# Which engines follow the source's order in the first attention: TensorE alone, or TensorE and ScalarE

## The chip, the cores and the metric

The kernel runs on one core of a Trainium2 chip. A core has a matrix engine (TensorE, PE in the profile), a vector engine (VectorE, DVE), a scalar engine (ScalarE, ACT), a general engine (GpSimd, POOL), and a queue that issues transfers (SyncE, SP). Each engine takes its own instructions in one fixed order and meets the others through semaphores. The metric is the device time of one execution in microseconds (us), smaller is better; the kernel before takes 1862.88 us, the median of three runs (1862.3 to 1863.4).

## What is computed

The reference is a block of four layers over `x` of 4 x 512 x 512. The change lies in the first: layer norm, then attention with 16 heads of 32, rotated and normalised queries and keys, and a residual.

```python
x = x + _L0_attn_ref(_layernorm(x), W_qkv, W_o)       # first attention
x = x + _L0_ffn_ref(_layernorm(x), w1, w3, w2)        # weights made ternary
x = x + _L1_attn_ref(_layernorm(x), ...)              # a state-space scan
x = x + _L1_ffn_ref(x, ...)                           # attention, then experts

# _L0_attn_ref
q = q * cos + _rotate_half(q) * sin ; q = _rms_norm(q)   # the same for k
scores = einsum('bhqd,bhkd->bhqk', q, k) / sqrt(D)       # causal
out = einsum('bhqk,bhkd->bhqd', softmax(scores), v)
return einsum('btc,oc->bto', out, W_o)

# _L0_ffn_ref
s = mean(abs(w)) ; w1q = clip(round(w / s), -1, 1) * s   # also w3, w2
```

## The kernel before

Everything is one function, `block_kernel`, fully unrolled. A scheduler orders the instructions of each engine from the source and an estimate of its own of when each becomes ready; inside `tc.manual_schedule(engines=...)` the named engines keep the order of the source instead. The first attention stands in such a block (L400) that names TensorE alone; the three later blocks of this kind are not touched.

The first attention goes over four sequences `b`. For each:

- `norm` and `turn_in`: VectorE makes the normalised `row` (L123) of a tile of 128 tokens, TensorE transposes it (`tp`, L132), ScalarE copies it out to `hT` (L133).
- `project(b, t, s)`, for 4 tiles `t` and `s` = 0, 1, 2 for queries, keys and values: eight matmuls in the profile, `pq` (L284). Values are copied out by ScalarE (`v`, L289). Queries and keys go through a chain over three engines: VectorE makes `rot` (L296, two instructions) and `qk` (L300), GpSimd adds them (L303), ScalarE squares the sum (`sqk`, L305), VectorE sums the squares (`qkss`, L306).
- `scale_heads(b, i)`: nine small VectorE instructions for the inverse roots (L312 to L323) and two large multiplications (L325), for two tiles.
- `turn_heads(b, t)`: two transposes (`tp`, L132) that ScalarE copies out to `qkT` (L133).
- `attend(b, between)`: 16 steps `m`. A step has `scores` (matmuls `sc`, L359, into two PSUM pairs; ScalarE's two exponentials `pt`, L364; GpSimd's causal mask, L365), then what `between[m]` lists, then `weigh` of the step before (matmuls `av` and `sm`, L377). After every fourth `weigh` VectorE takes a reciprocal `r` (L385) and makes `oT` (L386).
- `back(b, t)`: the output projection `y` (L340) and the residual (L343).

The two PSUM pairs serve one step's scores, so the scores of step m+1 start when the exponentials of step m have read them. Four further banks serve `pq`, `tp`, `y`, `av` and `sm` in turn.

`between` spreads other work over the steps of `attend(b)`: the `back` of sequence b-1 in steps 1 to 4, the projections of b+1 in steps 0 and 5 to 15, `scale_heads` in 9 and 14, `turn_heads` in 12 and 13, and one *job* on the feed-forward weights at most. A job is a measurement by ScalarE (sum of absolute values: `measure`, L234, for w1 and w3; `measure_down`, L252, for w2) or a quantisation by VectorE (`quantize`, L201 and L202). The measurements of w1 belong to steps 1, 3, ..., 15 of `attend(0)`, quantisations of w1 and measurements of w2 alternate in `attend(1)`, the rest of w2 and w3 is measured in `attend(2)`, w3 is quantised in `attend(3)`. All pieces go through two buffers `q_w`; each job issues the transfer of the piece two jobs later on SP (L218), which waits for its buffer. The list of jobs, and so SP's order, is fixed by the source.

The opening, ahead of `attend(0)`, is:

```python
norm(0, 2)
for i in range(2):
    turn_in(0, i)
    for t in (2 * i, 2 * i + 1):
        project(0, t, 0)
        project(0, t, 1)
    scale_heads(0, i)
```

then the four value projections and `turn_heads` of sequence 0, and `norm(1)`, `turn_in(1, ...)`.

Of the kernel before, what the change touches and what calls it, by code (L numbers as in the profile page):

```python
# [46 lines left out]
def block_kernel(ctx: ExitStack, tc: tile.TileContext, a: dict, out: bass.AP):  # L47
# [116 lines left out]
    with tc.tile_pool(name="a_w", bufs=1) as aw, tc.tile_pool(name="a_1", bufs=1) as a1, tc.tile_pool(  # L164
# [65 lines left out]
        def measure(name, n):  # L230
            def job(raw):
                if n == 0:
                    parts[name] = const.tile([P, 2 * NK], F32, tag="q_" + name, name="q_" + name)
                nc.scalar.activation(raw, raw, AF.Abs, accum_out=parts[name][:, n : n + 1])  # L234

            jobs.append((half(name, n), job))
# [29 lines left out]
        def norm(b, pieces=1):  # L266
            normed[b] = []
            layer_norm(a1, xs[b], lambda t, op: normed[b].append(op), pieces)
            inputs_T[b] = a1.tile([P, NK, T], F32, tag="hT", name="hT")
            heads[b] = a1.tile([P, NT, 2 * H, D], F32, tag="qk", name="qk")  # L270
            squares[b] = a1.tile([P, NT, 2 * H], F32, tag="qkss", name="qkss")
            turned_qk[b] = a2.tile([P, 2 * NG, T], F32, tag="qkT", name="qkT")
            values[b] = a2.tile([P, NT, C], F32, tag="v", name="v")

        def turn_in(b, i):
            for t in (2 * i, 2 * i + 1):
                row = a2.tile([P, C], F32, tag="row", name="row")
                normed[b][t](row)
                transpose_into(inputs_T[b], row, t * P)

        def project(b, t, s):
            y = bank("pq")
            for k in range(NK):
                nc.tensor.matmul(  # L284
                    y, inputs_T[b][:, k, t * P : (t + 1) * P], wqkv[:, k, s * C : (s + 1) * C],
                    start=k == 0, stop=k == NK - 1,
                )
            if s == 2:
                nc.scalar.copy(values[b][:, t, :], y)  # L289
                return  # L290

            src = y.rearrange("p (h d) -> p h d", d=D)
            dst = heads[b][:, t, s * H : (s + 1) * H, :]
            rot = a2.tile([P, H, D], F32, tag="rot", name="rot")
            for i in range(2):
                nc.vector.tensor_tensor(  # L296
                    rot[:, :, i::2], src[:, :, 1 - i :: 2],
                    sin[:, t, i::2].unsqueeze(1).to_broadcast([P, H, D // 2]), ALU.mult,
                )
            nc.vector.tensor_tensor(  # L300
                dst, src, cos[:, t, :].unsqueeze(1).to_broadcast([P, H, D]), ALU.mult
            )
            nc.gpsimd.tensor_tensor(dst, dst, rot, ALU.add)  # L303
            sq = a2.tile([P, H, D], F32, tag="rot", name="sqk")
            nc.scalar.activation(sq, dst, AF.Square)  # L305
            nc.vector.tensor_reduce(squares[b][:, t, s * H : (s + 1) * H], sq, AX.X, ALU.add)  # L306

        def scale_heads(b, i):
            rs = a1.tile([P, 2, 2 * H], F32, tag="ri_qk", name="ri_qk")
            v = a1.tile([P, 2, 2 * H], F32, tag="ri_v", name="ri_v")  # L310
            u = a1.tile([P, 2, 2 * H], F32, tag="ri_u", name="ri_u")
            nc.vector.tensor_scalar(  # L312
                v, squares[b][:, 2 * i : 2 * i + 2, :], 1.0 / D, QK_EPS, ALU.mult, ALU.add
            )


            nc.vector.tensor_scalar(
                rs.bitcast(I32), v.bitcast(I32), -0.5, float(0x5F3759DF), ALU.mult, ALU.add
            )
            for _ in range(3):  # L320
                nc.vector.scalar_tensor_tensor(u, rs, -0.5, v, ALU.mult, ALU.mult)
                nc.vector.tensor_tensor(u, u, rs, ALU.mult)
                nc.vector.scalar_tensor_tensor(rs, u, 1.5, rs, ALU.add, ALU.mult)  # L323
            for t in (2 * i, 2 * i + 1):
                nc.vector.tensor_tensor(  # L325
                    heads[b][:, t], heads[b][:, t],
                    rs[:, t - 2 * i, :].unsqueeze(2).to_broadcast([P, 2 * H, D]), ALU.mult,
                )

        def turn_heads(b, t):  # L330
            flat = heads[b][:, t].rearrange("p h d -> p (h d)")
            for s in range(2):
                transpose_into(
                    turned_qk[b][:, s * NG : (s + 1) * NG, :], flat[:, s * C : (s + 1) * C], t * P
                )
# [61 lines left out]
        def do(f, *args):  # L397
            return lambda: f(*args)

        with tc.manual_schedule(engines={mybir.EngineType.PE}):  # L400

            norm(0, 2)
            for i in range(2):
# [6 lines that stand above are left out]
                project(0, 2 * i, 2)  # L410
                project(0, 2 * i + 1, 2)
                turn_heads(0, 2 * i)
                turn_heads(0, 2 * i + 1)
            norm(1)
            turn_in(1, 0)
            turn_in(1, 1)
            w3 = None

            for n in range(2 * NK):
                measure("w1", n)  # L420
            at_step = {(0, 1 + 2 * n): n for n in range(2 * NK)}
            scale_at = {(1, 0): "w1", (2, 10): "w2", (3, 0): "w3"}
            for n in range(2 * NK):
                at_step[1, 1 + 2 * n] = len(jobs)
                quantize(lambda: w1, "w1", n)
                at_step[1, 2 + 2 * n] = len(jobs)
                measure_down(n)
            for n in range(2 * NK):
                if n + 2 * NK < NF:
                    at_step[2, 1 + 2 * n] = len(jobs)  # L430
                    measure_down(n + 2 * NK)
                at_step[2, 2 + 2 * n] = len(jobs)
                measure("w3", n)
            for n in range(2 * NK):
                at_step[3, 1 + 2 * n] = len(jobs)
                quantize(lambda: w3, "w3", n)
            fetch_piece()
            fetch_piece()
            w3 = None
            for b in range(B):  # L440
                between = {m: [] for m in range(18)}
                if b > 0:
                    for t in range(NT):
                        between[1 + t].append(do(back, b - 1, t))
                if b + 1 < B:
                    n = b + 1
                    order = [(0, 0), (0, 1), (1, 0), (1, 1), (0, 2), (2, 0), (2, 1), (1, 2)]
                    order += [(3, 0), (3, 1), (2, 2), (3, 2)]
                    for m, (t, s) in zip([0] + list(range(5, 16)), order):
                        between[m].append(do(project, n, t, s))  # L450
                    between[9].append(do(scale_heads, n, 0))
                    between[12].append(do(turn_heads, n, 0))
                    between[13].append(do(turn_heads, n, 1))
                    between[14].append(do(scale_heads, n, 1))

                for m in range(17):
                    if (b, m) in scale_at:
                        between[m].append(do(find_scale, scale_at[b, m]))
                    if (b, m) in at_step:
                        between[m].append(do(next_job, at_step[b, m]))  # L460
                if b == B - 1:
                    first_mv = const.tile([P, NT, 2], F32, tag="mv", name="mv")
                    for t in range(NT):
                        between[9].append(do(statistics, a1, xs[0], t, first_mv))
                attend(b, between)
                if b + 1 < B:
                    turn_heads(b + 1, 2)
                    turn_heads(b + 1, 3)
                if b + 2 < B:
                    norm(b + 2)  # L470
                    turn_in(b + 2, 0)
                    turn_in(b + 2, 1)
                if b + 2 == B:
                    w3 = place("w3")
            for t in range(NT):
                back(B - 1, t)
# [589 lines left out]
    with tc.tile_pool(name="c_1", bufs=1, reuse_waits="tile") as c1, tc.tile_pool(  # L1066
# [82 lines left out]
        engines = {getattr(mybir.EngineType, e) for e in ("PE", "DVE", "Activation", "Pool", "SP")}  # L1149
# [334 lines left out]
    with tc.tile_pool(name="e_1", bufs=1, reuse_waits="tile") as e1, tc.tile_pool(  # L1484
# [255 lines left out]
        engines = {mybir.EngineType.PE, mybir.EngineType.DVE, mybir.EngineType.Activation}  # L1740
# [64 lines left out]
```

## Time and profile before

One execution was profiled: it took 1863.49 us, of which the span from the first to the last instruction is 1861.8 us.

| stretch (us from the span's start) | what runs | length | TensorE busy | ScalarE busy | VectorE busy |
|---|---|---|---|---|---|
| 0 to 40 | loads and the opening | 40.0 | 28.7 | 10.5 | 26.6 |
| 40 to 80 | rest of the opening, first steps of attend(0) | 40.0 | 37.3 | 21.6 | 21.2 |
| 320 to 360 | end of attend(2) | 40.0 | 38.9 | 15.1 | 20.5 |
| 360 to 400 | attend(3) | 40.0 | 38.4 | 15.3 | 24.8 |
| 400 to 1861.8 | the other three layers | 1461.8 | 1386.3 | 786.2 | 903.1 |

"Busy" is the time in which the engine executes; the granted TensorE clock is listed apart, 1.00 being full speed. In the timelines, an engine's idle time and what ended it stand in brackets behind the first instruction after it. Over the whole span GpSimd is busy for 568.4 us (31%).

### The profile page before, as it was taken

The page shows a single profiled execution, that of the slowest core. Times are in us where ns is not written, and L with a number is a line of the kernel's source. Part 1 is how long each engine was busy: PE and PEld are TensorE (multiplying, and loading weights), DVE is VectorE, ACT ScalarE, POOL GpSimd, SP SyncE. Part 2 cuts the span into 40 slices and gives each one's busy share as a digit, 9 for nine tenths or more (in the row PEclk, how much of TensorE's full clock was granted, in tenths as well). Part 3 has the DMA queues.
Part 4 walks back from the last instruction along what each step waited for, and adds up shares of the span by engine and source line. Part 5 has one row for each costly group of instructions (what it writes and reads, how often), then busy time and mean ns, then how long its engine had stood idle before and what let it go on. Part 6 is the DMA issues. An engine that isn't in the chain of part 4 may idle for free.

```text
span 1861.8 us, 27452 instructions
## 1 busy us (share of the span) xinstructions
PE 1757.1 (94%) x10374; PEld 1094.2 (59%) x10374; DVE 1123.3 (60%) x1812; ACT 938.3 (50%) x1940; POOL 568.4 (31%) x383
## 2 busy tenths in 40 slices
PE   7999999999999998899997989999999999999998
PEld 3434343436777766788886875656556554544444
DVE  6456545557656556999888886574766764222222
ACT  2433442332243526989989867675676652011111
POOL 3221212120112020889887860100000000244441
PEclk9999999999999999999999987999999999999999
DMA  7002300102001122323223200000010007455545
GB/s 245 20 1 72 104 1 1 29 18 71 10 28 43 57 80 68 103 94 104 57 63 112 58 28 1 1 24 1 1 35 24 24 24 246 132 91 91 91 80 141
DMA packets 74630, 115.07 MB, mean 62 GB/s; under 512 B 9546, under 2 KB 34762, under 8 KB 73940
## 3 DMA queue, kind: packets, MB, share of 16 engines
q1 hardware_dynamic: 64996, 90.87, 15.2%
q0 software_dynamic: 8656, 20.32, 6.1%
q8 instruction: 83, 1.36, 0.3%
q10 hardware_dynamic: 848, 2.13, 0.3%
q14 instruction: 47, 0.39, 0.1%
HBM read 83.02 MB, written 33.42 MB: 63 GB/s over the span
## 4 chain that ended last, share of the span: by engine, by line
PE 66%; ACT 10%; DVE 9%; issue 2%; DMA 2%; POOL 1%; DVEq 0%; ACTq 0%; POOLq 0%
PE pgr L1684 7%; PE pg L826 7%; PE ys L1135 4%; PE scd L1369 4%; PE yr L1705 4%; PE pq L284 3%; PE bu L1103 3%; PE y L1309 3%; PE y L844 3%; PE pge L1270 3%; PE bu L1098 3%; PE tpd L1392 2%; PE y L340 2%; ACT pr L1380 2%; PE tp L132 2%
## 5 line engine op out<-in xcount | busy, mean ns | idle before, releaser
L1122 POOL TENSOR_TENSOR hc<-h,cb 128x1024 f32<-128x1024 f32 x128 | 301.3, 2380 | 110.2 <-DVE h L1111 91.0
L1111 DVE TENSOR_TENSOR_SCAN h<-da,bu 128x512 f32<-128x512 f32 x256 | 294.9, 1203 | 24.6 <-PE bu L1103 10.5
L284 PE MATMUL pq<-wqkv,hT 128*128 128x512 f32 x384 | 179.6, 615 | 1.5 <-ACT hT L133 1.5
L1091 ACT ACTIVATE da<-delta_l,am 128x511 f32<-128x511 f32 x256 | 163.4, 709 | 2.4 <-DVE h L1111 2.4
L1380 ACT ACTIVATE pr<-scd,nm 128x128 f32<-128x128 f32 (+3 forms) x256 | 133.4, 531 | 57.4 <-DVE nm L1377 56.2
L826 PE MATMUL pg<-hTh,w 128*128 128x512 f32 (+1 forms) x352 | 146.2, 415 | 1.4 <-ACT hTh L813 0.7
L826 PE MATMUL pg<-hTl,w 128*128 128x512 f32 (+1 forms) x352 | 140.6, 400 | 0.2 <-DVE hTl L814 0.2
L1135 PE MATMUL ys<-ident,hc 128*128 128x128 f32 x1024 | 137.2, 278 | 3.2 <-DVE h L1111 1.4
L1103 PE MATMUL bu<-ident,bu 128*128 128x128 f32 x768 | 132.2, 279 | 7.8 <-ACT bu L1085 7.7
L1684 PE MATMUL pgr<-wgu,gTe 128*128 x304 | 137.1, 593 | 0.0
L1085 ACT ACTIVATE bu<-dxT,bts 128x512 f32<-128x512 f32 x192 | 124.4, 712 | 13.0 <-PE bu L1103 12.6
L284 PEld LDWEIGHTS pq<-wqkv,hT 128*128 128x128 f32 x384 | 71.5, 194 | 94.2 <-issue 84.8
L364 ACT ACTIVATE pt<-sc 128x1024 f32<-128x1024 f32 (+3 forms) x128 | 84.1, 698 | 83.5 <-PE sc L359 81.0
L1369 PE MATMUL scd<-kTd,qTd 32*128 32x512 f32 (+3 forms) x512 | 108.9, 505 | 14.4 <-ACT pr L1380 11.5
L1135 PEld LDWEIGHTS ys<-ident,hc 128*128 128x128 f32 x1024 | 119.3, 144 | 4.4 <-DVE h L1111 1.6
L1098 PE MATMUL bu<-diag_l,dxT 128*128 128x128 f32 x512 | 105.6, 289 | 14.0 <-DVE h L1111 10.3
L1377 DVE TENSOR_REDUCE nm<-scd 128x2 f32<-128x256 f32 (+3 forms) x128 | 105.0, 821 | 2.8
L1392 PE MATMUL tpd<-ident,pr 128*128 128x128 f32 x640 | 102.5, 291 | 2.7 <-ACT hTr L133 0.9
L1098 PEld LDWEIGHTS bu<-diag_l,dxT 128*128 128x128 f32 x512 | 81.7, 195 | 37.1 <-DVE h L1111 19.7
L365 POOL TENSOR_SCALAR_AFFINE_SELECT pt<-pt 128x512 f32<-128x512 f32 x64 | 43.5, 679 | 195.3 <-ACT pt L364 195.3
L1103 PEld LDWEIGHTS bu<-ident,bu 128*128 128x128 f32 x768 | 95.3, 145 | 12.0 <-ACT bu L1085 11.9
L1392 PEld LDWEIGHTS tpd<-ident,pr 128*128 128x128 f32 x640 | 75.3, 146 | 36.4 <-issue 23.0
(337 smaller groups left out, 3182.3 us busy)
## 6 DMA issues: line engine op xcount, KB each, us to landing
cb<-c_rows SPq DMA_DIRECT2D x64, 256.0 KB, 3.2
q_w<-in_w2T SPq DMA_DIRECT2D x20, 256.0 KB, 2.7
diag_l<-diags SPq DMA_DIRECT2D x64, 64.0 KB, 1.9
hrows<-h SPq DMA_DIRECT2D x4, 1024.0 KB, 4.3
acc<-x SPq DMA_DIRECT2D x16, 256.0 KB, 2.0
wgu<-in_r_gate SPq DMA_DIRECT2D x7, 512.0 KB, 9.3
wgu<-in_r_up SPq DMA_DIRECT2D x7, 512.0 KB, 10.0
wdn<-in_r_down SPq DMA_DIRECT2D x7, 512.0 KB, 9.4
```

What stands on the lines that cost most here:

```text
L284: nc.tensor.matmul(y, inputs_T[b][:, k, t * P : (t + 1) * P], wqkv[:, k, s * C : (s + 1) * C], start=k == 0, stop=k == NK - 1,)
L826: nc.tensor.matmul(pg[:rows, i, :], w[:, k, f * P : f * P + rows], part[:, k, :], start=k + m == 0, stop=k + m == NK,)
L1091: nc.scalar.activation(da[:, k, 1:], delta[:, k, 1:], AF.Exp, scale=am[:, k, n : n + 1])
L1098: nc.tensor.matmul(bu[:, :P], loaded[b][1][:, 0, k * P : (k + 1) * P], scaled[b, n][0], start=True, stop=True,)
L1103: nc.tensor.transpose(bu[:, t * P : (t + 1) * P], scaled[b, n][t][:, k * P : (k + 1) * P], ident)
L1111: nc.vector.tensor_tensor_scan(h[:, i, :], decays[b, n][:, 2 * half + i, :], bu, 0.0, ALU.mult, ALU.add)
L1122: nc.gpsimd.tensor_tensor(hc, states.pop((b, n, half)), weighed[b, n].unsqueeze(1).to_broadcast([P, 2, T]), ALU.mult)
L1135: nc.tensor.matmul(sums[b][t][:, k * P : (k + 1) * P], hc[:, i, t * P : (t + 1) * P], ident, is_transpose=True, start=n == 0 and k == 0, s ...
L1369: nc.tensor.matmul(sc[:, i, :w], qT[at, g, t * P : w], kT[at, g, :w], start=True, stop=True)
L1380: nc.scalar.activation(pr[:, i, :w], sc[:, i, :w], AF.Exp, bias=nm[:, i : i + 1], accum_out=sums[b, g][:, t, 2 * p + i : 2 * p + i + 1],)
L1392: nc.tensor.transpose(tp[:, j * P : (j + 1) * P], pr[:, i, j * P : (j + 1) * P], ident)
L1684: nc.tensor.matmul(pg, gT[:, k, :], wgu[:, bass.ds(e, 1), k, :].rearrange("p e o -> p (e o)"), start=k == 0, stop=k == NK - 1,)
```

## The change

ScalarE is added to the engines that keep the source's order in the first attention.

```diff
-        with tc.manual_schedule(engines={mybir.EngineType.PE}):
+
+
+        engines = {mybir.EngineType.PE, mybir.EngineType.Activation}
+        with tc.manual_schedule(engines=engines):
```

No instruction is added or removed, and TensorE's, GpSimd's and SP's orders are the same in both programs, line for line. ScalarE's order differs in its first 220 instructions, VectorE's in its first 310, all of them of the first attention. What moves on ScalarE:

- In the opening, the fourth `sqk` now stands ahead of the second pair of `hT` copies (before: three squares, the two copies, a measurement, then the fourth square). The eight measurements of w1 and the first of w2, which lay between the opening's squares, move to their steps: w1 to `attend(0)`, w2 to `attend(1)`.
- In every step with a projection of queries or keys, `sqk` stands ahead of the next step's two `pt` (before: often between the two, or behind).
- In steps 12 and 13, `sqk` stands ahead of the two `qkT` copies of `turn_heads` (before: behind them).
- In `attend(1)`, the measurements of w2 and w3, which stood close together between the exponentials, are one to every second step; those of w3 and the last of w2 move to `attend(2)`.

On VectorE, the inverse roots of the first `scale_heads` are no longer mixed with rotations, and quantisations of w1 are spread over `attend(1)`. Some PSUM banks are handed on otherwise: in steps 12 and 13 the second `tp` takes the bank of the projection just read by VectorE, and the next projection waits for the copy of the first `tp`.

## The prediction

> **What bounds the kernel.** The change can only act where the first attention runs, so I read a table of stretches first, one row for each of `attend(0)`, `attend(1)` and `attend(2)`, cut where their first scores begin. Columns: start and end, length, busy time and (instructions) of PE, PEld, DVE, ACT, POOL, then granted clock, DMA share, GB/s.
>
> ```profile
> 63.37:151.38 88.01, 83.37 (x529) 34.55 (x528) 47.44 (x80) 34.60 (x57) 22.38 (x25) 1.00 0.00 1
> 151.38:263.38 112.00, 104.11 (x564) 42.94 (x563) 63.88 (x107) 46.94 (x92) 22.19 (x25) 0.95 0.25 73
> 263.38:359.84 96.46, 93.93 (x547) 38.43 (x546) 43.95 (x73) 32.24 (x53) 21.18 (x24) 1.00 0.00 1
> ```
>
> TensorE is busy for 93 to 97% of each; no other engine passes 57%. So TensorE is the bound, and what counts is where it stands idle. `attend(1)` and `attend(2)` hold the same projections and `back` calls, yet differ by 15.54 us and in clock. 3.0 of that is the `turn_in` that only `attend(1)` is followed by (148.44 to 151.46 for the same transposes after `attend(0)`). **12.5 us are lost in `attend(1)`.** Next, what TensorE waited for up to 415 us (total, times, longest):
>
> ```profile
> PE sc L359 <- ACT pt L364: 9.6, 8, 2.9
> PE tp L132 <- ACT qkT L133: 3.2, 8, 0.7
> PE sm L377 <- DVE r L385: 2.8, 2, 1.4
> ```
>
> The two longest of the first row are in `attend(1)`: 178.66 to 181.58 and 208.01 to 210.84. ScalarE's timeline at the first shows what it did instead of exponentials:
>
> ```profile
> 175.36 0.63 ACT L252 ACTIVATE q_w<-q_w 128x512 f32<-128x512 f32 x1 [3.16 <-DVE q_u L201]
> ...
> 179.90 0.63 ACT L252 ACTIVATE q_w<-q_w 128x512 f32<-128x512 f32 x1 [3.81 <-DMA q_w<-in_w2T]
> 180.43 0.19 ACT L252 ACTIVATION_READ_ACCUMULATOR q_w<-q_w 128x1 f32 x1
> 180.53 1.92 ACT L364 ACTIVATE pt<-sc 128x1024 f32<-128x1024 f32 x2
> ```
>
> It sat idle for 3.81 us in front of a measurement whose piece had not landed, with the scores (ended 174.45) waiting behind it. At 208 it is the same with w3. After both, the clock falls:
>
> ```profile
> 177.00:180.40 3.40, 1.66 (x19) 0.57 (x17) 1.86 (x4) 0.50 (x1) 0.00 (x0) 1.00 0.53 180
> ...
> 183.90:187.30 3.40, 3.40 (x6) 1.33 (x5) 3.36 (x4) 2.12 (x4) 0.57 (x1) 0.50 0.32 67
> ...
> 207.80:211.20 3.40, 0.57 (x10) 0.30 (x4) 1.19 (x4) 2.71 (x5) 0.00 (x0) 1.00 0.63 174
> 211.20:214.60 3.40, 3.07 (x9) 1.00 (x6) 3.09 (x10) 3.40 (x8) 0.64 (x1) 0.50 0.56 165
> 214.60:218.00 3.40, 3.40 (x5) 1.35 (x4) 3.40 (x3) 0.49 (x1) 1.49 (x1) 0.50 0.25 89
> ```
>
> **Part 1, removed: the stalls of `attend(1)`, -12.5 us.** In source order one measurement (0.63 + 0.19) stands in every second step, so its piece, issued two jobs (two steps, over 8 us) ahead and 2.9 to 3.1 us on its way, is there; and the exponentials are no longer behind several. Idle 2.9 + 2.8; half clock for 3.4 and 6.8 us, which costs half of them, 5.1; the remaining 1.7 are scores paced by late exponentials (1.83 and 3.3 us where 1.14 is usual), partly offset since `attend(1)` was spared the 1.4 us wait for `r` of the third row, which comes back. What is late next is priced in part 4.
>
> The eight measurements of w1 (0.77 + 0.19) go from the opening's idle time into `attend(0)`, the rest of w2 and w3 into `attend(2)`. ScalarE is busy there for 34.6 of 88 and 32.2 of 96.5 us; a step lasts 5 to 6 us, its ScalarE work (two `pt` of 1.0 at most, `sqk`, one measurement, two `qkT` at times) under 5. I cost them at nothing; were that cover gone, each would cost 0.9. SP's order is the same, each job's transfer is only issued later, and nothing needed soon stands behind them: the next on SP are weights of the second layer.
>
> **Part 2, added: the opening, +5.5 us.**
>
> ```profile
> 27.57 0.63 ACT L305 ACTIVATE sqk<-qk 128x512 f32<-128x512 f32 x1 [3.37 <-POOL qk L303]
> ...
> 28.10 1.07 ACT L133 ACTIVATE hT<-tp 128x512 f32<-128x512 f32 x2
> ...
> 28.73 4.99 PE L284 MATMUL pq<-wqkv,hT 128*128 128x512 f32 x11 [1.47 <-ACT hT L133]
> ...
> 30.26 1.50 POOL L303 TENSOR_TENSOR qk<-qk,rot 128x512 f32<-128x512 f32 x1 [1.53 <-DVE qk L300]
> ...
> 31.79 0.63 ACT L305 ACTIVATE sqk<-qk 128x512 f32<-128x512 f32 x1 [1.87 <-POOL qk L303]
> ```
>
> Today the `hT` copies come after the third square, and TensorE resumes at 28.73. Now they stand behind the fourth, which can't start before 31.79: VectorE's and GpSimd's orders ahead of it are unchanged. So 31.79 + 0.63 + 0.59 (one copy) = 33.0, and TensorE, which has only projections queued that read `hT`, is idle from 27.27 to 33.0: 4.3 us more. 5.7 us idle is twice the idles above, so a half-clock run of 3.4 to 6.8 us follows; it begins within the idle, I take 4.2 us of it behind the restart, 2.1 more. The 0.9 us that TensorE waits at 50.48 behind a `v` copy goes: VectorE's inverse roots and two L325 now run unmixed from 33.2 to 38.4, the last square, by a chain of 4.0 us a projection (0.76 + 0.68 + 1.27 + 0.63 + 0.69) from there, ends by 53.4, before TensorE needs that copy (57). 4.3 + 2.1 - 0.9.
>
> **Part 3, added: squares in front.** In `attend(0)` step 1 there is no `back` to cover: `sqk` ends at 71.64, then both `pt` (0.8 each), so the second half of the next scores starts at 73.25 instead of 72.39: **+0.9**. In `attend(1)` and (2), step 1 has 3.7 us of `back` there: nothing. In steps 5 to 11 the square is done 3.5 us after its projection, the `pt` behind it by 6, and the scores that need them start after 7.5 or more: nothing; with that cover gone, 1 to 2 us a step.
>
> Steps 12 and 13, in `attend(0)`:
>
> ```profile
> 125.53 0.60 ACT L133 ACTIVATE qkT<-tp 128x512 f32<-128x512 f32 x1 [2.07 <-PE tp L132]
> ...
> 126.18 0.66 PE L132 MATMUL tp<-ident,qk 128*128 128x128 f32 x4 [0.69 <-ACT qkT L133]
> ...
> 127.90 0.63 ACT L305 ACTIVATE sqk<-qk 128x512 f32<-128x512 f32 x1 [0.44 <-POOL qk L303]
> ```
>
> Now `qkT` follows the square: 128.53 + 0.6 = 129.1. The second `tp` takes another bank (free at 126.5, +0.4), but the next projection waits for the first `qkT`: 129.1 instead of 128.19. In step 13 the same chain (rotation from 132.8, GpSimd to 135.6, square to 136.2, copy to 136.7) holds the step 14 projection to 136.8 instead of 135.20. So **1.6 us** in each of three sequences, **+4.8**.
>
> **Part 4, added: the last piece of w1, +4.3 us.** In `attend(1)` the sixth measurement of w2 stands behind the step 12 `qkT`: 5.3 us after projection 12 ends. Only then does SP issue the next two transfers, 0.33 apart: the last piece of w1 lands at about 5.3 + 0.5 + 2.9 = 8.7. VectorE's fixed order has its quantisation (0.58 + 0.93) ahead of step 13's rotation, which so ends (0.76 + 0.68) at 11.8 rather than 9.2; `qkT` follows at 14.3, not 11.7: 2.6 us. TensorE is idle there for about 2.2 + 0.8. Whether such an idle costs clock is where **the Trainium skill and the trace differ**. "TensorE: Matmul & The Clock Gate", Part 1, has the clock fall only after a whole idle window of about 3.4 us: by it nothing. In the rows above a stretch with 1.66 us of 3.40 busy, and an idle of 2.9, was followed by half clock. I take the trace: one run of 3.4, +1.7. By the rule the total is 1.7 lower. Bounds for the part: 0 (the piece lands early) and 6 (two runs).
>
> **Sum:** -12.5 + 5.5 + 0.9 + 4.8 + 4.3 = **+3.0 us**. On the profiled run that is 1863.5 + 3.0; the median shown is 0.6 lower, so I forecast 1865.9, and a span of 1864.8. The layers behind start later by the same amount. Bounds of the unknown terms: opening half clock 0 to 3.4 (2.1 taken, from the two runs shown), part 4 as said; together about -0.5 to +6.
>
> **Rivals.**
> - *ScalarE blocks more often than I traced* (slower). An engine in source order holds its exponentials behind every square, so each rotation delayed by a reciprocal (3.36 us on VectorE) becomes a TensorE stall. For: the waits list has VectorE and ScalarE idle for the rotation chain over 40 us each. Against: the margins of part 3. Six such steps at 1 us: 1872.
> - *The clock windows behind fall better* (faster). Mean clock from 400 us to the end is 0.98, so about 4% of 1462 us, 58 us or 17 runs of 3.4, go at half; a later start moves the same short idles against those windows. Each run that drops out saves 1.7, so from four on the result is faster: 1859. For: runs follow idles of under 3 us. Against: it may as well add some, and three runs agree within 1.1 us.
> - *The order on the chip doesn't change.* Excluded: the compiled orders differ.
>
> **Chances.** Forecast 0.55, the blocking rival 0.32, the clock rival 0.13. About 0.2% (3.7 us) can't be told from no change: 1859.2 to 1866.6. The forecast lies near the upper edge: of its 0.55, 0.33 the same and 0.22 slower; the clock rival gives 0.10 faster, 0.03 the same. So faster 0.10, same 0.36, slower 0.54. Range 1860 to 1873, about a tenth outside at each end.
>
> **What would show it.** Right: `attend(1)` some 8 us shorter with a clock near 1.00; TensorE idle from 27 to 33 behind `hT`; a wait of projections for `qkT` three times; half clock shortly after 30. Wrong: a shift of the restart of under 3 us; rows of scores waiting for exponentials in steps 5 to 11; VectorE not waiting for w1's last piece; a changed clock behind 400.

## The result and the profile after

The changed kernel takes **1867.86 us** (median of 7 runs, 1866.4 to 1869.1), the kernel before 1862.67 us beside it: a ratio of 1.0027, 95% interval 1.0018 to 1.0037, which is 5.0 us (3.4 to 6.9) lost. A second set of 15 runs in a later session gave 1.0025 (1.0015 to 1.0036). The profiled execution took 1866.38 us, its span is 1864.7 us.

Three rows of the table of stretches of the changed kernel, cut as before at the first scores of `attend(0)`, `attend(1)` and `attend(2)` (start and end, length, busy time and instructions of PE, PEld, DVE, ACT, POOL, granted clock, DMA share, GB/s):

```profile
68.78:160.60 91.82, 85.11 (x530) 34.91 (x529) 47.60 (x81) 39.74 (x73) 22.25 (x25) 0.98 0.11 30
160.60:265.87 105.27, 98.20 (x563) 40.74 (x562) 64.53 (x106) 38.58 (x72) 22.16 (x25) 0.98 0.16 47
265.87:363.93 98.06, 94.05 (x547) 38.42 (x547) 44.01 (x74) 39.41 (x75) 21.10 (x24) 1.00 0.13 37
```

Set against the rows of before, these rows and the opening give the account up to the second layer:

| part | before | after | difference | predicted |
|---|---|---|---|---|
| opening, to the first scores of attend(0) | 63.37 | 68.78 | +5.41 | +5.5 |
| attend(0) | 88.01 | 91.82 | +3.8 | +2.5 |
| attend(1) | 112.00 | 105.27 | -6.7 | -6.6 |
| attend(2) | 96.46 | 98.06 | +1.6 | +1.6 |
| attend(3), to the first matmul of the next layer | 72.43 | 72.70 | +0.3 | 0 |
| sum | 432.27 | 436.63 | +4.4 | +3.0 |

The change gains in one stretch and pays in three. ScalarE is busy for 5 and 7 us longer in `attend(0)` and `attend(2)`, where the measurements went, and 8 us less in `attend(1)`. The +0.3 of `attend(3)` is one wait of scores for exponentials, 0.87 us instead of 0.60.

What TensorE waited for up to 415 us (total, times, longest), in the changed kernel:

```profile
PE pq L284 <- ACT hT L133: 5.1, 1, 5.1
PE sm L377 <- DVE r L385: 5.1, 3, 2.4
PE sc L359 <- ACT pt L364: 4.5, 5, 1.5
PE tp L132 <- DVE qk L300: 3.5, 3, 1.2
PE pq L284 <- ACT qkT L133: 3.1, 6, 0.7
PE sm L377 <- DVE qk L300: 1.5, 1, 1.5
```

The waits of scores for exponentials have halved (9.6 to 4.5 us). The first row (the opening) has grown from 1.5 to 5.1 us and that of `r` from 2.8 to 5.1; new are rows four and five (steps 12 and 13 of three sequences: one wait for VectorE and two for a copy in each) and the last (behind w1's last piece).

The opening, from the timeline of the changed kernel (start, duration; in brackets the idle time before it and what ended it):

```profile
27.30 0.63 ACT L305 ACTIVATE sqk<-qk 128x512 f32<-128x512 f32 x1 [3.37 <-POOL qk L303]
...
29.99 1.49 POOL L303 TENSOR_TENSOR qk<-qk,rot 128x512 f32<-128x512 f32 x1 [1.53 <-DVE qk L300]
31.52 0.63 ACT L305 ACTIVATE sqk<-qk 128x512 f32<-128x512 f32 x1 [3.58 <-POOL qk L303]
32.05 1.07 ACT L133 ACTIVATE hT<-tp 128x512 f32<-128x512 f32 x2
...
32.68 1.22 PE L284 MATMUL pq<-wqkv,hT 128*128 128x512 f32 x1 [5.12 <-ACT hT L133]
```

ScalarE does nothing for 3.58 us, with the copies of finished transposes queued behind a square that waits for GpSimd; TensorE, which needs the copies, starts at 32.68 instead of 28.73.

And the two idles of TensorE in `attend(1)` that the change brought, from the same kernel's timeline:

```profile
205.53 1.26 POOL L303 TENSOR_TENSOR qk<-qk,rot 128x512 f32<-128x512 f32 x1 [1.64 <-DVE qk L300]
205.53 1.63 DVE L201 TENSOR_SCALAR q_u<-q_w,sc_w 128x683 f32<-128x683 f32 x1
...
214.69 3.34 DVE L385 RECIPROCAL r<-sm 128x512 f32<-128x512 f32 x1
...
218.09 1.06 PE L377 MATMUL sm<-pt,ones 128*32 128x512 f32 x8 [2.35 <-DVE r L385]
...
244.33 0.58 DVE L201 TENSOR_SCALAR q_u<-q_w,sc_w 128x682 f32<-128x682 f32 x1 [0.74 <-DMA q_w<-in_w1T]
...
247.28 0.64 PE L377 MATMUL sm<-pt,ones 128*32 128x512 f32 x4 [1.47 <-DVE qk L300]
```

The second comes with w1's last piece, as forecast: VectorE waits 0.74 us for it, and the quantisation stands in front of the rotation that `sm` waits for. The first is larger than the 1.4 us known from before: a quantisation now stands in front of the inverse roots and took 1.63 us where the other took 0.58, so the reciprocal behind them started late. In the 1.26 us from its start GpSimd was adding a rotation (L303); the last section has more on this.

### The profile page after: what moved, and what is told of

The parts are those of the page before. It is cut to its first block, busy times and chain, and to the rows that moved or that the text cites. A ratio compares the mean times of both kernels' runs of the same rounds, so it can differ in the third digit from the quotient of the medians.

```text
span 1864.7 us, 27435 instructions
## 1 busy us (share of the span) xinstructions
PE 1752.6 (94%) x10374; PEld 1092.6 (59%) x10374; DVE 1123.5 (60%) x1812; ACT 935.4 (50%) x1940; POOL 567.7 (30%) x383
## 4 chain that ended last, share of the span: by engine, by line
PE 71%; DVE 12%; ACT 10%; issue 3%; DMA 2%; POOL 2%; SPq 0%; DVEq 0%; ACTq 0%; POOLq 0%
PE pq L284 7%; PE pgr L1687 7%; PE pg L829 6%; PE ys L1138 4%; PE yr L1708 4%; PE scd L1372 3%; PE bu L1106 3%; PE y L1312 3%; PE y L847 3%; PE y L340 3%; PE pge L1273 3%; PE bu L1101 3%; PE tpd L1395 2%; PE sc L359 2%; ACT pr L1383 2%
## 5 line engine op out<-in xcount | busy, mean ns | idle before, releaser
L1101 PE MATMUL bu<-diag_l,dxT 128*128 128x128 f32 x512 | 106.2, 290 | 15.8 <-DVE h L1114 12.7
```

The source lines that it names most:

```text
L1101: nc.tensor.matmul(bu[:, :P], loaded[b][1][:, 0, k * P : (k + 1) * P], scaled[b, n][0], start=True, stop=True,)
```

## The experiments

All are compared with the kernel before, on the same chip in the same session (its medians there were 1860.32, 1860.52 and 1862.82 us). The medians of one kernel move by 2 us and more between sessions, so the stretches of the traces carry most of the weight: equal code gives equal stretches to within 0.3 us (a second profile of the changed kernel: 91.77, 105.21 and 98.07), but for a run of half clock that comes or stays away, some 1.5 to 1.7 us. Each row has the stretches of one execution and the ratio of all runs, so the two need not agree to a few us.

| kernel | opening | attend(0) | attend(1) | attend(2) | to next layer | against before | ratio (95%) |
|---|---|---|---|---|---|---|---|
| before | 63.37 | 88.01 | 112.00 | 96.46 | 432.27 | | 1 |
| changed | 68.78 | 91.82 | 105.27 | 98.06 | 436.63 | +4.4 | 1.0027 (1.0018 to 1.0037) |
| opening by the scheduler | 63.52 | 91.84 | 103.59 | 98.06 | 433.06 | +0.8 | 1.0003 (0.9990 to 1.0017) |
| attentions by the scheduler | 68.51 | 88.02 | 110.83 | 96.46 | 437.94 | +5.7 | 1.0041 (1.0028 to 1.0054) |
| transposes of h in front | 64.80 | 91.78 | 105.17 | 98.06 | 432.51 | +0.2 | 1.0034 (1.0021 to 1.0046) |
| the same, second time | 66.15 | 90.28 | 105.11 | 98.06 | 434.00 | +1.7 | 1.0008 (0.9996 to 1.0021) |
| transposes of q in front | 68.68 | 94.41 | 105.40 | 99.87 | 444.41 | +12.1 | 1.0080 (1.0066 to 1.0093) |
| jobs in front | 68.80 | 91.90 | 101.82 | 98.06 | 433.01 | +0.7 | 1.0001 (0.9992 to 1.0010) |
| squares later | 68.58 | 87.20 | 100.20 | 96.46 | 426.80 | -5.5 | 0.9984 (0.9974 to 0.9993) |
| ScalarE ordered in attend(1) alone | 62.94 | 88.01 | 106.03 | 98.34 | 429.45 | -2.8 | 0.9987 (0.9979 to 0.9995) |
| opening by the scheduler, squares later | 63.59 | 87.20 | 102.02 | 96.46 | 425.31 | -7.0 | 0.9963 (0.9951 to 0.9975) |
| the same, jobs in front | 63.67 | 86.66 | 100.65 | 96.47 | 421.58 | -10.7 | 0.9932 (0.9915 to 0.9949) |

"To next layer" includes `attend(3)`, 72.4 to 72.7 us where no half clock falls into it, 74.1 to 74.4 with one run of 3.4 us and 76.0 with two.

### Each half of the change alone

The opening with TensorE alone in source order, the rest with ScalarE too:

```diff
+        first_two = {mybir.EngineType.PE}
-        with tc.manual_schedule(engines=engines):
+        with tc.manual_schedule(engines=first_two):
             norm(0, 2)
             ...
+        with tc.manual_schedule(engines=engines):
             norm(1)
```

> ScalarE in source order from the first attention on, but in the opening only TensorE is. Sum of parts: the opening goes back to before's (TensorE restarts near 28.7 us, first scores of attend(0) near 63.4 instead of 68.8), attend(0) to attend(2) keep what they have in the changed kernel (about 92, 105, 98 us). So -5.4 us against the changed kernel: 1862.5 us, level with the kernel before. ScalarE blocking elsewhere: the opening gains less than 3 us or attend(0) gives it back, because measurements of w1 stay there. Clock windows: stretches behind 436 us move by more than 2 us in spite of an unchanged order, and the sum is off by that much.

The opening is back at 63.52 us, a gain of 5.3, and `attend(0)` to `attend(2)` keep their lengths, all but 1.7 us of `attend(1)`, where a run of half clock is missing (below). In `attend(3)` two such runs came, which cost 3.4 us. The total is level with before. So the opening's cost is the opening's order and nothing that it hands on.

The other half: `first_two` names both engines, the rest TensorE alone.

> ScalarE in source order in the opening only; the attentions have TensorE alone in source order, as before. Sum of parts: the opening keeps the cost if the fourth square still stands ahead of the hT copies (first scores of attend(0) near 68.8 us), attend(0) is back at 88 us, attend(1) at about 112 us with its two idles of near 3 us behind w2 and w3 measurements and half clock after them, attend(2) at 96.5. Total before + 5.4: 1868 us, level with the changed kernel. If the gain of attend(1) comes from elsewhere than the order of its measurements, attend(1) stays near 105 us here, and the total is near 1861.

The opening costs its 5.1 us, `attend(0)` and `attend(2)` are those of before, and `attend(1)` has its stalls again. The row of `attend(1)` in this kernel, with ScalarE's 47.03 us and the clock at 0.95 as before:

```profile
156.53:267.36 110.83, 103.71 (x563) 42.90 (x563) 63.83 (x107) 47.03 (x92) 22.15 (x25) 0.95 0.24 74
```

The two halves of the change don't touch each other: what the opening loses is 5.1 here and 5.4 in the changed kernel, and the attentions' +3.8, -6.7 and +1.6 come and go with ScalarE's order in them.

### Both transposes of h in front

```diff
             norm(0, 2)
             for i in range(2):
                 turn_in(0, i)
+            for i in range(2):
                 for t in (2 * i, 2 * i + 1):
```

> The changed kernel with both transposes of h ahead of the opening's projections, so that the hT copies stand in front of the squares on ScalarE. Sum of parts: TensorE has no idle of 5.1 us at 27.6, and not the half clock from 31 to 38 behind it: first scores of attend(0) 6.5 us earlier, near 62.3 us, and 1861.4 us in all. Rival: the projections then come earlier than squares and rotations can take them, and the wait moves to the end of the opening (first scores not before 66 us; total above 1865).

The idle at 27.6 went, as forecast, and 2.5 of the 6.5 us came back at the end of the opening, at the transposes of q (timeline of this kernel):

```profile
49.15 0.63 PE L132 MATMUL tp<-ident,qk 128*128 128x128 f32 x4 [1.27 <-DVE qk L300]
...
51.63 1.73 PE L132 MATMUL tp<-ident,qk 128*128 128x128 f32 x7 [1.85 <-ACT v L289]
```

Half clock follows (50.9 to 54.3). The chain of rotations and squares needs its time; TensorE that comes earlier waits there. The total of 1.0034 doesn't fit a trace that is 4.1 us ahead of the changed kernel's at the next layer; the profiled execution was 4.3 us faster than the median of its ten runs. A second set of runs:

> The same kernel as that with both transposes of h in front, a second time: its first FFN matmul came at 432.5 us, 4.1 before the changed kernel's, yet its total was 1.0034 of the kernel before. If that total comes from clock windows behind 432 us that go with the kernel's phase, the ratio is near 1.003 again and the mean granted clock under that of the kernel before; if it was chance, the ratio is near 1.000.

1.0008, below the first interval: the first total didn't repeat. The mean granted clock of those ten runs was 0.9796, that of the kernel before beside them 0.9811: an estimated 2.8 us (0.0015 of 1865) of the 6 us by which they are slower went to half clock. Where, and why in that session, isn't known. In the second profile the opening is at 66.15, where the rival began. Of its 6.5 us the edit gives 2.6 to 4.0.

### Transposes of q in front

```diff
+                    between[12].append(do(turn_heads, n, 0))
+                    between[13].append(do(turn_heads, n, 1))
                     for m, (t, s) in zip([0] + list(range(5, 16)), order):
                         between[m].append(do(project, n, t, s))
                     between[9].append(do(scale_heads, n, 0))
-                    between[12].append(do(turn_heads, n, 0))
-                    between[13].append(do(turn_heads, n, 1))
```

> The changed kernel with the transposes of q (turn_heads) ahead of the projection in steps 12 and 13, so that the qkT copies no longer stand behind that projection's square. Sum of parts: the six waits of projections for qkT (3.1 us) and the 1.6 us a sequence go: attend(0), (1), (2) each shorter by about 1.6, together -4.8, total 1863. Rival: the transposes come before their input is ready and TensorE waits for the scaling of q instead; then each sequence is as long as now or longer, total 1868 or more.

The expectation failed: 7.8 us worse than the changed kernel up to the next layer, 4.5 in the first three attentions and 3.4, by half clock, in the fourth. The rival's direction was right, its mechanism not: TensorE doesn't wait for the scaling but for the copies (timeline of this kernel):

```profile
136.52 0.63 ACT L305 ACTIVATE sqk<-qk 128x512 f32<-128x512 f32 x1 [6.11 <-POOL qk L303]
137.05 1.49 ACT L364 ACTIVATE pt<-sc 128x768 f32<-128x768 f32 x2
138.43 1.09 ACT L133 ACTIVATE qkT<-tp 128x512 f32<-128x512 f32 x2
...
139.08 0.70 PE L284 MATMUL pq<-wqkv,hT 128*128 128x512 f32 x1 [2.96 <-ACT qkT L133]
```

The transposes end at 136.12, the projection needs one of their banks, and between the two stand on ScalarE the square of the projection before, which waits for the rotation, and two exponentials. The projection had been the cover of that chain; with the transposes directly ahead of it there is none.

### Squares later

Three squares of each sequence are written apart from their projection, with `measure_heads` holding L305 and L306; `project` gets a switch for it (not shown), and the rest is untouched.

```diff
-                        between[m].append(do(project, n, t, s))
+                        between[m].append(do(project, n, t, s, m not in (0, 12, 13)))
+                    between[1].append(do(measure_heads, n, 0, 0))
-                    between[12].append(do(turn_heads, n, 0))
-                    between[13].append(do(turn_heads, n, 1))
+                    between[12] += [do(turn_heads, n, 0), do(measure_heads, n, 3, 0)]
+                    between[13] += [do(turn_heads, n, 1), do(measure_heads, n, 3, 1)]
```

> The changed kernel with three squares of each sequence written later: that of step 0 behind step 1's exponentials, those of steps 12 and 13 behind the qkT copies. The order of TensorE is the same. Sum of parts: the whole of part 3 goes: attend(0) 88.0 us (the wait of 1.5 us at 76 and the half clock behind it go as well), attend(1) about 103.7, attend(2) 96.5, total -7 against the changed kernel, near the kernel before or 2 us below it. Rival: the 1.6 us a sequence have another source (VectorE's order, which stays): attend(2) stays near 98 us and the total gains less than 4 us.

Its rows of `attend(0)` to `attend(2)`:

```profile
68.58:155.78 87.20, 83.12 (x529) 34.55 (x528) 47.65 (x81) 40.19 (x73) 22.19 (x25) 1.00 0.11 32
155.78:255.98 100.20, 96.29 (x563) 40.12 (x562) 65.43 (x106) 39.01 (x72) 22.32 (x25) 1.00 0.16 50
255.98:352.44 96.46, 93.94 (x547) 38.43 (x546) 44.10 (x74) 39.87 (x75) 21.06 (x24) 1.00 0.13 38
```

`attend(2)` is to 0.01 us that of before, with the measurements still in it (ScalarE 39.87 against 32.24): they cost nothing there, and the 1.6 us are the place of two squares. `attend(0)` is 0.8 us shorter than before, since even there a square stood between two exponentials. `attend(1)` gains 5.1 us: the 1.6, the half clock (none follows here), and the idle of 1.47 behind w1's last piece, which is absent from this trace; 4.8 by these terms. That piece was late because its request hung on a measurement behind `qkT` copies behind a square. **So the late piece follows from part 3.** The wait for `r` does not: it is still 2.19 us here, and that no half clock follows it goes with where the idle falls on the grid of half-clock runs (last section).

### Jobs in front

```diff
-                        between[m].append(do(next_job, at_step[b, m]))
+                        between[m].insert(0, do(next_job, at_step[b, m]))
```

> The changed kernel with each step's piece of work on w1, w2, w3 (measurement, quantisation, fetch of the next) ahead of that step's projections instead of behind them. Sum of parts: the measurement of w2 in step 12 no longer stands behind that step's qkT copies, the last transfers of w1 go out some 3 us earlier, and the idle of 1.5 us behind w1's last quantisation (245.8 to 247.3 in the changed kernel) goes: attend(1) 103.8 instead of 105.3, the other stretches as they are, total -1.5. Rival: quantisations ahead of rotations on VectorE delay the rotations and with them squares and exponentials in several steps: attend(1) 107 or more.

`attend(1)` is 3.5 us shorter, more than the 1.5 expected. VectorE's timeline of this kernel shows the rest:

```profile
201.61 0.57 DVE L201 TENSOR_SCALAR q_u<-q_w,sc_w 128x683 f32<-128x683 f32 x1 [1.57 <-DMA q_w<-in_w1T]
...
213.84 3.35 DVE L385 RECIPROCAL r<-sm 128x512 f32<-128x512 f32 x1
```

The quantisation fills VectorE's wait ahead of the rotation, takes 0.57 us there, and the reciprocal starts 0.85 us earlier (with the kernel itself 0.1 later). TensorE waits 1.40 us for `r` instead of 2.35, and no half clock follows. The idle behind w1's last piece is gone as well, so the terms come to 0.95 + 1.7 + 1.47 = 4.1, of which 3.5 show; what takes the rest isn't shown. Both waits go with the place of the job in its step.

### Versions that beat both kernels

ScalarE in source order in `attend(1)` alone, where it gains, by an inner block (`tensor` names TensorE, `both` TensorE and ScalarE):

```diff
-                attend(b, between)
+                with tc.manual_schedule(engines=both if b == 1 else tensor):
+                    attend(b, between)
```

> ScalarE in source order in attend(1) alone; opening, attend(0), attend(2) and attend(3) have TensorE alone in source order, as before. Sum of parts: first scores of attend(0) at 63.4, attend(0) 88.0, attend(1) near 104 instead of 112, attend(2) 96.5: 8 us less than the kernel before, ratio about 0.996. Rival: the measurements of w3 that attend(1) no longer takes are packed by the scheduler ahead of copies or exponentials of attend(2), and 3 to 6 us come back as waits for a piece behind 265 us.

2.8 us up to the next layer instead of 8. `attend(1)` is 106.03, with a half-clock run and two new waits of 1.0 and 0.4 us for `qkT` at its end, where measurements stand among the copies on ScalarE, as the rival had it for `attend(2)`; that is 1.9 longer than before, and a run of half clock in `attend(3)` takes another 1.7.

The opening by the scheduler with the squares later:

> The opening with TensorE alone in source order, all attentions with ScalarE too, and the squares of steps 0, 12 and 13 written later as in the kernel above. Sum of parts: first scores of attend(0) at 63.5, attend(0) 88.0, attend(1) near 102, attend(2) 96.5, attend(3) 72.5: 10 us less than the kernel before, ratio about 0.995. If the clock windows decide, the gain up to the first FFN matmul is 10 us but the total moves by less than 6 or more than 14.

7.0 us up to the next layer, with half clock in `attend(3)` (76.0 us instead of 72.4); without it the parts add to 10.6, for the 10 expected. With the jobs in front as well:

> The kernel of the last run (opening with TensorE alone, squares later) with each step's piece of work on the weights ahead of its projections as well. Sum of parts: the wait for r of 2.35 us in attend(1) shrinks to 1.4 and the half clock behind it (209.8 to 213.2) goes: attend(1) about 99.3 instead of 102.0, the rest as it is, ratio to the kernel before about 0.995. Rival: what the job order gained in the changed kernel came from the square ahead of the qkT copies, which is gone here already: attend(1) stays at 101 or more and the ratio at 0.996.

```profile
63.67:150.33 86.66, 82.77 (x530) 34.27 (x529) 47.60 (x81) 40.18 (x73) 22.34 (x25) 1.00 0.12 32
150.33:250.98 100.65, 96.57 (x563) 40.16 (x562) 64.46 (x106) 39.02 (x72) 23.37 (x25) 1.00 0.18 50
250.98:347.45 96.47, 93.93 (x547) 38.43 (x546) 44.04 (x74) 39.65 (x75) 21.14 (x24) 1.00 0.13 38
```

The clock is 1.00 in all three. TensorE's waits for `r` up to 360 us (L390 is L385 of before):

```profile
PE sm L382 <- DVE r L390: 4.2, 3, 1.4
PE tp L132 <- DVE r L390: 0.8, 1, 0.8
```

The wait of 2.35 us is down to 1.4 and the half clock behind it is gone; `attend(1)` gains 1.4 us, not 2.7, so the rival had half of it; the new wait of 0.8 us at a transpose takes part. **The ratio is 0.9932 (0.9915 to 0.9949), median 1850.58 us of six runs: 12.7 us less than the kernel before by the ratio.** 10.7 of these are in the trace up to the next layer, in spite of one run of half clock in `attend(3)`; the other 2 lie within what the medians move by.

The changed kernel was run once more beside it:

> The changed kernel itself, beside the two others on one chip: 4.4 us more than the kernel before up to the first FFN matmul, ratio 1.002 to 1.003 if the rest of the program takes the same time in both; the first scores of attend(0) to attend(3) within 0.5 us of those of its first profile.

1.0025, and its four first scores at 69.09, 160.87, 266.07 and 364.14 us, within 0.3 of the first profile's.

## Why the prediction was right, and where its terms were off

The forecast was 1865.9 us in a range of 1860 to 1873, with "slower" the likeliest; the runs gave 1867.86. The sum up to the next layer was +3.0 and is +4.4; behind it the ratio leaves +0.6 us, with an interval of some 2 to either side, which can't be told from nothing. The mechanism holds: one stretch gains, and the opening and steps 12 and 13 lose for the reasons given. That `attend(1)` came out within 0.1 us is in part luck, by part 4.

- **Part 1, the stalls of attend(1), holds.** The idles of 2.9 and 2.8 us are gone, and idles of 2.4 and 3.0 come back when the attentions are left to the scheduler (110.83). For the part itself 12.4 us are left once the 1.6 of part 3 and the 4.1 of part 4 are set aside. The measurements are free where they went: `attend(2)` with squares later shows it.
- **Part 2, the opening, holds: +5.4 for +5.5.** The restart moved by 3.95 us (4.3 forecast), half clock lasted from 31.3 to 38.1, 5.5 us of it behind the restart (4.2 forecast, so 2.7 and not 2.1 lost), and the wait for `v` went.
- **Part 3, steps 12 and 13, holds: 1.6 a sequence.** In step 1 of `attend(0)` the matmuls `av` behind the wait came 0.7 us later (0.9 forecast). **The term that was missing is the clock there:** the idle of 1.54 us was given none, and half clock from 79.1 to 82.5 cost another 1.5. This is the whole difference between +2.5 and +3.8.
- **Part 4 had the right size in the wrong place.** Forecast were a delay of 2.6 us behind w1's last piece and one run of half clock, 1.7. The idle is 1.47 us and no half clock follows. In its stead the wait for `r` grew by 0.95, and the half clock follows that. 1.47 + 0.95 + 1.7 is 4.1 for the 4.3 forecast, and that these agree is luck. That a quantisation would move in front of the inverse roots was to be had from VectorE's compiled order, and I hadn't followed it there.
- **The clock rule.** The prediction set "TensorE: Matmul & The Clock Gate", Part 1, of the Trainium skill (a whole idle window of about 3.4 us) against the trace, and took the trace. Idles of 1.54 and 2.35 us were followed by half clock, so one run behind a short idle was right to count. One of 1.47 was not, so neither gives the place. The row taken as the trace's word was misread: between the stretch with 1.66 us busy and the half clock lies one at full clock, with TensorE busy for 2.32 us.
- **The rivals.** "ScalarE blocks more often than I traced" would have shown as scores waiting for exponentials in steps 5 to 11 of the first three attentions: none over 0.3 us but one of 0.59 in step 5 of `attend(0)`, which was 0.60 before. Of "the clock windows behind fall better" the mean clocks show nothing: 0.9806 for the kernel before (27 runs) and 0.9800 for the changed kernel (15 runs) in one session.
- **The bounds of the sum** were put at -0.5 to +6. With the bounds given for its terms (0 for the 2.1 of the opening and for the 4.3 of part 4) the lower end is -3.4.

That stretch of the kernel before, in front of the half clock from 183.9 us:

```profile
180.40:183.90 3.50, 2.32 (x10) 0.92 (x11) 0.42 (x2) 2.04 (x4) 0.64 (x1) 1.00 0.58 174
```

That the clock in `attend(1)` would be near 1.00 was not met (0.98), through the one run behind `r`.

## What to carry to other kernels

An engine held to the source's order can pay wherever the source writes a consumer of a slow chain ahead of ready work and nothing covers the wait. In steps 5 to 11 the squares cost nothing; in the opening, in step 0 of `attend(0)` and in steps 12 and 13 they did, and three stretches lost 10.8 us against a gain of 6.7 in the fourth. Before giving the order up, list what each instruction on that engine waits for and write the late ones later: with the opening left to the scheduler, three squares written later and the weight work written first in each step, source order was 12.7 us faster than the kernel before. And count a chain across engines: a square ahead of a copy delayed a measurement, its transfer, a quantisation, and a rotation in the next step.

## What the runs showed of the hardware

**The clock.** The same idle of TensorE may or may not cost a run of half clock. All half-clock runs of a profile begin whole multiples of 3.41 us apart, so a profile can be cut into stretches of that length, here called its grid. In step 1 of `attend(0)` TensorE stood idle for 1.54 us between the same instructions in seven profiles. In five of them half clock followed (the changed kernel twice, the opening by the scheduler, jobs in front, and the transposes of h in front the first time); in the second profile of the last and with the transposes of q in front none did. Two neighbouring stretches of 3.4 us in the changed kernel:

```profile
75.67:79.07 3.40, 1.86 (x16) 0.60 (x8) 0.69 (x1) 2.65 (x5) 1.27 (x2) 1.00 0.00 0
79.07:82.47 3.40, 3.39 (x26) 1.11 (x24) 0.00 (x0) 1.11 (x4) 0.73 (x2) 0.50 0.40 108
```

and the two of the kernel with the transposes of q in front, cut on the grid of its own half-clock runs (30.5 and 139.7 us are 32 times 3.41 apart):

```profile
74.87:78.27 3.40, 1.86 (x17) 0.43 (x8) 0.69 (x1) 1.95 (x4) 1.27 (x1) 1.00 0.00 0
78.27:81.67 3.40, 3.39 (x46) 1.45 (x44) 0.00 (x0) 2.34 (x7) 1.27 (x2) 1.00 0.36 108
```

Both have TensorE busy for 1.86 of 3.40 us and then full, and the clock is 0.50 in one and 1.00 in the other. So busy time alone doesn't decide. They differ in what TensorE did: score matmuls (L359) make up 1.26 us of the first and 0.57 of the other. In the second profile with the transposes of h in front a boundary of the grid divides the idle, with TensorE busy for 2.74 us on one side and 2.54 on the other.

With the wait of 2.2 to 2.35 us for `r` in `attend(1)` it is where the idle falls on the grid. It stands in nine profiles, and half clock follows in seven. The changed kernel, and the opening by the scheduler, where none follows:

```profile
215.60:219.00 3.40, 1.05 (x12) 0.16 (x8) 3.40 (x4) 0.00 (x0) 0.00 (x0) 1.00 0.00 0
219.00:222.40 3.40, 3.40 (x15) 1.63 (x12) 2.13 (x5) 0.00 (x0) 1.19 (x1) 0.51 0.27 77
```

```profile
207.80:211.20 3.40, 2.70 (x12) 0.55 (x11) 3.40 (x3) 0.00 (x0) 0.65 (x1) 1.00 0.05 18
211.20:214.60 3.40, 1.75 (x17) 0.58 (x18) 3.40 (x5) 0.00 (x0) 0.00 (x0) 1.00 0.00 0
```

In the first the idle lies within one stretch, in the second a boundary divides it. In the seven profiles TensorE is busy for 1.06 to 1.52 us of such a stretch, in the two without half clock (this one and squares later) for 1.81 and 1.85.

Counted over the stretches of all thirteen profiles that ran at full clock, from 10 to 428 us: behind the 17 with TensorE busy for less than 1.58 us half clock followed every time, behind the 1408 with more than 2.57 never. Of the 115 in between it followed in 16, all of them among the 26 with more than 0.95 us of score matmuls. These limits are read off these traces, and the amount of score matmuls was not varied by itself; why the other 10 of the 26 kept full clock stays open. An idle of this length should be priced at its own time, with 1.7 us more as one end of the range.

**The quantisation beside GpSimd.** L201 took 1.63 us at 205.53 in the changed kernel and 0.57 at 201.61 with the jobs in front. GpSimd's addition L303 ran beside the first and not beside the second. The thirteen profiles hold 104 such quantisations of w1. In 22 of them L303 was running or began within 0.05 us; these took 1.12 to 1.68 us and ended 0.37 us behind it. The other 82 took 0.65 us at most. In two of those L303 began 0.06 and 0.07 us behind L201, and then it was L303 that took 1.6 us instead of 1.27. The two orders were not varied by themselves, but they come with the changed kernel's wait for `r`: a quantisation right behind a rotation meets that rotation's addition.
